# Queries and keys as further columns of the values' projection, brought to their rows through DRAM

## The chip, the core and the metric

The kernel runs on one core of a Trainium2 chip. A core has TensorE (PE: matmuls, with its weight loads listed as PEld), VectorE (DVE), ScalarE (ACT), GpSimd (POOL) and SyncE (SP, which here only issues DMAs), a 128-partition SBUF, and PSUM with 8 banks, into which matmuls write. The metric is the device time of one execution in microseconds.

## What is computed

Two layers work on x of shape (4, 64, 96, 96) in fp32. The first is an attention over all 9216 positions of an image, with a sigmoid in place of a softmax; the second multiplies a few Fourier modes by weights. The change concerns the first.

```python
# layer 0, on xn = _gn(x); C = 64, C8 = 8, N = 96 * 96 = 9216
q = jnp.einsum('bchw,oc->bohw', xn, wq) + bq      # 8 channels
k = jnp.einsum('bchw,oc->bohw', xn, wk) + bk      # 8 channels
v = jnp.einsum('bchw,oc->bohw', xn, wv) + bv      # 64 channels
energy = jnp.einsum('bcn,bcm->bnm', Q, K)
att = jax.nn.sigmoid(energy)
out = jnp.einsum('bcm,bnm->bcn', V, att) + xn
scale = jax.nn.sigmoid(mlp(out.mean) + mlp(out.max))
x = x + out * scale
# layer 1
x = x + irfft2(modes of rfft2(_gn(x)), mixed over channels)
```

## The kernel before

The four images are worked on as two pairs; the channels of a pair's two images fill the 128 partitions of `xs[p]`. The positions of a pair are cut into 18 blocks of 512. Each block is in turn a query tile (512 columns), and against each query tile stand 144 tiles of keys: 72 groups of 128 positions for each of two images. So 2 x 18 x 144 = 5184 tiles are worked through, each in three steps: an energy matmul into one PSUM bank (L481), a sigmoid on ScalarE over three or four banks at a time (L500), and the values times these attentions on TensorE (L517).

**Rows of queries and keys.** An energy matmul contracts over 32 rows: 8 channels, four times, since each of query and key is split into a high and a low part so that products of fast-format numbers (float32r) give fp32 accuracy. Four such groups of 32 rows lie in 128 partitions (two images, twice). The projection matrices `wq` and `wk` have the 8 columns repeated so that a matmul puts them at once into all rows. `keys(p, s)` (L428) projects one block into a bank, and `halves` and `low_or_high` (L406, L407, L416) make the high part in some rows and the rest in others, into `kT`. `queries` (L452) does the same for a query tile, and copies halves to the other rows (L462). `values_of` (L439, L443) projects the values of a block with x as the stationary operand, into `vT`.

**Order.** A planner runs ahead of the work (`while len(done) < len(sizes)`) and cuts the tiles into bursts of seven (six where a bank is needed elsewhere). For each burst t it writes down which steps come with it: `together[t]` (projections, which use banks of the next burst that are free for a moment), `alone[t]` (one step with a bank of its own) and `ends[t]` (steps without a bank). The loop below then emits: the energies of burst t+1, the values for the older tiles, the sigmoids of burst t+1, some more values, the projections, the rest. The order on PE, ACT and DVE is this one by hand (`manual_schedule`); the order on SP's queue is left to the scheduler of the framework, and each queue works in order. SP's DMAs carry one of eight completion semaphores in turn, so that a DMA waits for the one eight before it.

Pair 0's keys and values are projected during its first query tile: `keys(0, s)` and `values_of(0, s)` come shortly before the energies of block s. Pair 1's are projected during the last query tile of pair 0, as the old keys and values are finished with (`renewed`). A query tile is projected 42 tiles ahead (`AHEAD`). During pair 1 the second layer of pair 0 is worked in between (`second_layer`, class `Hidden`), with many DMAs on SP's queue (L269 to L381). The tail is the second layer of pair 1.

Of the kernel before, what the change touches and what calls it, by code (L numbers as in the profile page):

```python
# [33 lines left out]
F32 = mybir.dt.float32  # L34
# [19 lines left out]

SIZE, HEAD = 7, 3
AHEAD = 6 * SIZE
ALL = NPAIR * NBLK * TILES
# [12 lines left out]

FIRST = {"wq": P, "wk": P, "wv": P, "pav": P, "bq": 1, "bk": 1, "low": 2, "nhalf": 1, "bv": P}
SECOND = {"w1": 2 * R, "w2": P, "ident": P, "fw": 2 * KW, "fh": 4 * KH, "gh": 2 * H, "gw": 4 * W}
# [11 lines left out]
def tile_kernel(ctx: ExitStack, tc: tile.TileContext, x, cst, late, spec, out):  # L84
# [24 lines left out]
    def named(name, rows=P):  # L109
        return cs[:rows, PLACE[name]]  # L110
# [273 lines left out]
    with tc.tile_pool(name="work", bufs=1) as work, \  # L384
# [10 lines left out]

        kT = kvp.tile([P, NCH // 2, P], F32R, tag="kT", name="kT")

# [3 lines left out]
        def halves(src, bias, name):  # L401

            shape = [P, src.shape[-1]]
            u = qp.tile(shape, F32, tag="full", name=f"full_{name}", bufs=1)
            h = qp.tile(shape, F32R, tag="high", name=f"high_{name}")
            nc.vector.tensor_scalar(u, src, bias, None, ALU.add)  # L406
            nc.vector.tensor_copy(h, u)  # L407
            return u, h
# [5 lines left out]
        def low_or_high(dst, u, h, is_low):  # L414

            mark[0] = nc.vector.scalar_tensor_tensor(dst, h.bitcast(F32), is_low, u,  # L416
                                                     ALU.mult, ALU.add)
# [5 lines left out]
        def keys(p, s):  # L423
            pp = bank_a(f"pk_{p}_{s}")
            src = xs[p][:, bass.ts(s, NB)].rearrange("p (a e m) -> p e a m", e=2, m=P)
            for e in range(2):
                cols = bass.ts(e, P // 2)
                projected[0] = nc.tensor.matmul(pp[cols, :NB // 2], named("wk")[:, cols],  # L428
                                                src[:, e, :, :], start=True, stop=True)
            ku, kh = halves(pp[:, :NB // 2], named("bk"), f"k_{p}_{s}")  # L430
            low_or_high(kT[:, 2 * s:2 * s + 2, :].rearrange("p a m -> p (a m)"), ku, kh,
                        low_sb[:, 1:2])

        def values_of(p, s):
            pp = bank_a(f"pv_{p}_{s}")

            for i in range(4):
                for e in range(2):
                    projected[0] = nc.tensor.matmul(  # L439
                        pp[bass.ts(e, P // 2), bass.ts(i, P)],  # L440
                        xs[p][:, bass.ts(2 * (4 * s + i) + e, P // 2)], named("wv"),
                        start=True, stop=True)
            nc.vector.tensor_tensor(  # L443
                vT[:, 4 * s:4 * s + 4, :], pp.rearrange("p (i m) -> p i m", m=P),
                named("bv").unsqueeze(1).to_broadcast([P, 4, P]), ALU.add)

        def queries(p, n):
            pq = bank_a(f"pq_{p}_{n}")
            half = NB // 2
            for e in range(2):  # L450
                rows = bass.ts(e, P // 2)
                projected[0] = nc.tensor.matmul(  # L452
                    pq[rows, :half], named("wq")[:, rows],
                    xs[p][:, n * NB + e * half:n * NB + (e + 1) * half], start=True, stop=True)
            qu, qh = halves(pq[:, :half], named("bq"), f"q_{p}_{n}")
            q = qp.tile([P, NB], F32R, tag="q", name=f"q_{p}_{n}")
            for e in range(2):
                rows, cols = bass.ts(e, P // 2), bass.ts(e, half)
                low_or_high(q[rows, cols], qu[rows, :], qh[rows, :], low_sb[rows, 0:1])
                for b in range(2):  # L460
                    to, of = 64 * (1 - e) + 32 * b, 64 * e + 32 * b
                    nc.vector.tensor_copy(q[to:to + 32, cols], q[of:of + 32, cols])  # L462
            return q
# [13 lines left out]
        def energies(t):  # L477

            for i in range(total[t] - sizes[t], total[t]):
                r = 32 * (i % 4)  # L480
                nc.tensor.matmul(banks[:, bank_of(i), :], kT[r:r + 32, i // 4 % (NCH // 2), :],  # L481
                                 ask[i // TILES][r:r + 32, :], start=True, stop=True)
# [4 lines left out]
        def parts(t):  # L487

            for lo, part in ((0, order[t][:HEAD]), (HEAD, order[t][HEAD:])):
                if part:  # L490
                    yield 7 * (t % 2) + lo, min(part), len(part)
# [93 lines left out]
        norm0[0]()  # L585
        norm0[1]()
        keys(0, 0)
        warm_behind()
        q = first_queries()
        warm_behind()  # L590
        values_of(0, 0)
        warm_behind()

# [73 lines left out]
        kept = [TILES * (NPAIR * NBLK - 1) + 2 * (STRIP // P) * (s + 1) for s in range(NSTRIP)]  # L667
        ask, asked, known, valued, renewed, again_at = {0: q}, 1, 2, 2, 0, 0
        sizes, total, order, done, block, edges = [6], [6], [list(range(1, 7))], [], [], set()
        way = 1  # L670
        while len(done) < len(sizes):

            t, was = len(done), done[-1] if done else 0
            n = max(1, -(-was // TILES))
            edge = TILES * n
            crossing = edge < ALL and edge < total[t] - 3
            block.append(n if crossing else n - 1)
# [12 lines left out]
            elif total[t] < ALL:  # L690
                steps = together.setdefault(t, [])
                while known < NBLK and known <= (total[t] + 2 * SIZE - 1) // 8:
                    steps.append(lambda s=known: keys(0, s))
                    if known + 1 < NBLK:
                        end(t, norm0[known + 1])
                    known += 1
                while valued < NBLK and valued <= (total[t] + 2 * SIZE - LAG) // 8:
                    steps.append(lambda s=valued: values_of(0, s))
                    valued += 1
                if renewed < NBLK and was >= TILES * (NBLK - 1) + 8 * (renewed + 1):  # L700
                    steps.append(lambda s=renewed: keys(1, s))
                    steps.append(lambda s=renewed: values_of(1, s))
                    renewed += 1
                if asked < NPAIR * NBLK and total[t] + AHEAD >= TILES * asked and t not in alone:
                    steps.append(lambda n=asked: ask.update({n: queries(n // NBLK, n % NBLK)}))
                    asked += 1
                assert len(steps) <= HEAD
                while chain and not steps and t not in alone:
                    own, step, wait, since = chain[0]
                    if t < max(ready[0] + wait, started[0] + since):  # L710
                        break
                    if own:
                        alone[t] = step
                    elif own is None:
                        end(t, step)
                    else:
                        steps.append(step)
                    ready[0] = t
                    chain.pop(0)
# [6 lines left out]
            if crossing:  # L726
                way = 1 if n % 2 else -1
            elif together.get(t - 1):
                way = -way
            order.append(list(free)[::way][:ALL - total[t]])  # L730
            sizes.append(len(order[-1]))
            total.append(total[t] + sizes[-1])
            done.append(total[-1] - LAG if crossing else min(edge, total[-1] - LAG))
            while again_at < NSTRIP and done[t] >= kept[again_at]:
# [9 lines left out]

        spare[0] = 0
        energies(0)
        sigmoids(0)
        later(norm0[2])
        keys(0, 1)
        warm_behind()  # L750
        values_of(0, 1)
        with tc.manual_schedule(engines=ENGINES):
            put_off = []
            for t in range(T):
# [9 lines left out]
                if t + 1 < T:  # L764
                    sigmoids(t + 1)
                at_work = next((i for i in range(old, len(items)) if sum(
                    c.stop - c.start for _, c in items[:i]) >= 2 * NB), len(items))
                attend(items[old:at_work])
                for i, step in enumerate(together.get(t, ())):
                    spare[0] = order[t + 1][i]  # L770
                    step()
# [192 lines left out]
def _constants(l0):  # L964
# [24 lines left out]
    for b in range(2):  # L989
        rows = slice(b * C, (b + 1) * C)  # L990
        a[rows, PLACE["wv"].start + b * C:PLACE["wv"].start + (b + 1) * C] = l0["wv"].T
        a[rows, PLACE["w1"].start + b * R:PLACE["w1"].start + (b + 1) * R] = l0["ca_w1"].T
        a[b * R:(b + 1) * R, PLACE["w2"].start + b * C:PLACE["w2"].start + (b + 1) * C] = \
            l0["ca_w2"].T
# [52 lines left out]
```

## Time and profile before

| What | Value |
|---|---|
| median of 3 runs | 3081.17 us (3081.09 to 3081.43) |
| the profiled execution | 3080.95 us, span 3079.2 us |
| granted TensorE clock, mean | 0.997 |
| L500 sigmoids, x1503 | 2394.5 us busy |
| L517 values times attentions, x11824 | 2408.3 us busy |
| L481 energies, x5040 (and x144 of the first tile) | 544.7 us (and 17.1) busy |
| queue q1 (SP): packets, MB | 72000, 71.57 |

A row of the groups gives the line of the code, the engine, the operation, what it writes and reads with shapes, how often it occurs, the busy time, the mean of one in ns, and the idle time of the engine just before such instructions with what ended it. An fp32 matmul is two records, and matmuls on different columns or rows of the array run at the same time, so busy time is less than count times mean. The timeline gives start, duration, engine and operation of merged instructions; SPq is SP's queue, where the duration of a DMA row is the time that SP needs to issue it, not that of the transfer. The first query tile ends at 134.9 us (the first row of L523) and the second at 214.92; the last one of pair 0 runs from 1406.30 to 1508.07.

### The profile page before, as it was taken

What the parts mean: (1) busy time and instruction counts of PE and PEld (TensorE: products, weight loads), DVE (VectorE), ACT (ScalarE), POOL (GpSimd) and SP (SyncE); (2) the same over time, 40 slices, a digit from 0 to 9 for tenths busy, and PEclk for the clock granted to TensorE, in tenths of its full rate; (3) what the DMA queues carried; (4) which work ended last, traced back from release to release, by engine and by line L of the source; (5) the groups of instructions that cost most, each with busy time, mean ns of one, the idle gap of its engine ahead of it and who ended that gap; (6) DMA issues with size and microseconds to landing.
All of it is one profiled execution on the core that took longest, in us unless ns stands there. A gap on an engine that the chain in (4) does not pass through costs nothing.

```text
span 3079.2 us, 42720 instructions
## 1 busy us (share of the span) xinstructions
PE 3055.0 (99%) x19022; PEld 1145.5 (37%) x19022; DVE 387.2 (13%) x818; ACT 2417.3 (79%) x1543; POOL 27.1 (1%) x52
## 2 busy tenths in 40 slices
PE   8999999999999999999999999999999999999998
PEld 4433333333333333334433333333333333333336
DVE  4300000000000000002312111100110000000005
ACT  4688888888888888887688887777777888888872
POOL 0000000000000000000000000000001000000001
PEclk9999999999999999999999999999999999999999
DMA  3000000000000000000122322412113000000027
GB/s 145 1 1 1 1 1 1 1 1 1 1 1 1 1 1 1 1 1 1 31 75 61 84 74 77 132 24 29 50 44 131 1 1 1 1 1 1 5 63 246
DMA packets 80490, 99.48 MB, mean 32 GB/s; under 512 B 48209, under 2 KB 58193, under 8 KB 80209
## 3 DMA queue, kind: packets, MB, share of 16 engines
q1 hardware_dynamic: 72000, 71.57, 8.0%
q0 software_dynamic: 5776, 20.45, 1.9%
q10 hardware_dynamic: 2528, 4.72, 0.4%
q8 instruction: 149, 2.44, 0.3%
q14 instruction: 37, 0.29, 0.0%
HBM read 67.49 MB, written 28.05 MB: 31 GB/s over the span
## 4 chain that ended last, share of the span: by engine, by line
PE 98%; DVE 1%; ACT 1%; DMA 0%; issue 0%; SPq 0%; DVEq 0%; ACTq 0%
PE banks L517 75%; PE banks L481 16%; PE banks L439 1%; PE banks L428 1%; PE banks L206 1%; PE banks L376 1%; ACT at L500 0%; PE banks L452 0%; PE py L955 0%; PE pv L206 0%; DMA x<-in_x_dram 0%; PE pa L857 0%; PE banks L354 0%; PE idle_I-15036_15051 L820 0%; PE pu L869 0%
## 5 line engine op out<-in xcount | busy, mean ns | idle before, releaser
L500 ACT ACTIVATE at<-banks 128x1536 f32<-128x1536 f32 x1503 | 2394.5, 1640 | 590.6 <-PE banks L481 564.3
L517 PE MATMUL banks<-at,vT 128*64 128x512 f32 (+1 forms) x11824 | 2408.3, 546 | 0.0
L517 PEld LDWEIGHTS banks<-at,vT 128*64 128x64 f32 x11824 | 780.3, 136 | 1338.6 <-issue 1280.1
L481 PE MATMUL banks<-q,kT 32*128 32x512 f32 x5040 | 544.7, 453 | 2.6 <-ACT at L500 2.5
L481 PEld LDWEIGHTS banks<-q,kT 32*128 32x128 f32 x5040 | 223.6, 183 | 453.8 <-ACT at L500 340.0
L406 DVE TENSOR_SCALAR full_q<-banks,cs 128x256 f32<-128x256 f32 x35 | 16.9, 483 | 1361.0 <-PE banks L452 1361.0
L523 DVE SCALAR_TENSOR_TENSOR x<-banks,x 128x512 f32<-128x512 f32 x36 | 24.9, 692 | 648.9 <-PE banks L517 648.9
L462 DVE CAST q<-q 32x256 fp32r<-32x256 f32 x140 | 39.9, 285 | 3.8
L439 PE MATMUL banks<-cs,x 128*64 128x128 f32 x576 | 37.7, 273 | 0.4 <-DVE at L471 0.4
L379 DVE TENSOR_TENSOR x<-banks,x 128x384 f32<-128x384 f32 x24 | 13.4, 558 | 188.0 <-PE banks L376 186.1
L439 PEld LDWEIGHTS banks<-cs,x 128*64 128x64 f32 x576 | 33.8, 137 | 7.3 <-issue 0.9
L416 DVE SCALAR_TENSOR_TENSOR q<-high_q,cs,full_q 64x256 fp32r<-64x256 f32 x70 | 33.6, 480 | 1.8
L406 DVE TENSOR_SCALAR full_k<-banks,cs 128x256 f32<-128x256 f32 x36 | 17.4, 484 | 115.6 <-PE banks L428 89.8
L443 DVE TENSOR_TENSOR vT<-banks,cs 128x512 f32<-128x512 f32 x36 | 24.7, 685 | 9.7 <-PE banks L439 9.7
L525 DVE TENSOR_REDUCE maxs<-x 128x1 f32<-128x512 f32 x36 | 24.7, 686 | 1.2
L619 DVE COPY ws<-banks 128x512 f32<-128x512 f32 x16 | 11.1, 692 | 95.7 <-PE banks L206 95.6
L531 DVE BATCH_NORM_STATS2 stats<-x 128x6 f32<-128x512 f32 x36 | 22.2, 680 | 6.0 <-DMA x<-in_x_dram 5.8
L428 PE MATMUL banks<-x,cs 128*64 128x256 f32 x144 | 22.3, 388 | 0.2 <-DVE x L152 0.2
L570 PE MATMUL banks<-x 128*128 128x256 f32 (+1 forms) x46 | 14.9, 470 | 6.3 <-DMA x<-in_x_dram 6.3
L452 PE MATMUL banks<-x,cs 128*64 128x256 f32 x140 | 21.1, 379 | 0.0
L481 PE MATMUL banks<-q_first,kT 32*128 32x512 f32 x144 | 17.1, 463 | 2.8 <-DVE kT L416 1.7
L376 PE MATMUL banks<-cs,ws 128*64 128x384 f32 x96 | 19.6, 486 | 0.0
(133 smaller groups left out, 467.8 us busy)
## 6 DMA issues: line engine op xcount, KB each, us to landing
ws<-in_spec_dram SPq DMA_DIRECT2D x20, 512.0 KB
x<-in_x_dram SPq DMA_DIRECT2D x14, 512.0 KB
room<-in_spec_dram SPq DMA_DIRECT2D x12, 512.0 KB
w<-in_spec_dram POOLq DMA_DIRECT2D x10, 512.0 KB, 6.8
old<-in_x_dram SPq DMA_DIRECT2D x12, 384.0 KB
x1d<-x SPq DMA_DIRECT2D x12, 384.0 KB
xd<-old SPq DMA_DIRECT2D x12, 384.0 KB
xT<-xd SPq DMA_DIRECT2D x36, 128.0 KB
```

The costliest lines, as they stand in the source:

```text
L206: self.last = nc.tensor.matmul(pv[bass.ts(g, 32), :].rearrange("q (n k o) -> q n k o", n=SIDE, o=C)[:, :, k, :], self.ut[:, at:at + 32], s ...
L376: nc.tensor.matmul(py[bass.ts(b, C), :4 * W], self.z[:, i, bass.ts(b, C)], named("gw"), start=True, stop=True)
L406: nc.vector.tensor_scalar(u, src, bias, None, ALU.add)
L416: mark[0] = nc.vector.scalar_tensor_tensor(dst, h.bitcast(F32), is_low, u, ALU.mult, ALU.add)
L428: projected[0] = nc.tensor.matmul(pp[cols, :NB // 2], named("wk")[:, cols], src[:, e, :, :], start=True, stop=True)
L439: projected[0] = nc.tensor.matmul(pp[bass.ts(e, P // 2), bass.ts(i, P)], xs[p][:, bass.ts(2 * (4 * s + i) + e, P // 2)], named("wv"), star ...
L443: nc.vector.tensor_tensor(vT[:, 4 * s:4 * s + 4, :], pp.rearrange("p (i m) -> p i m", m=P), named("bv").unsqueeze(1).to_broadcast([P, 4, P ...
L462: nc.vector.tensor_copy(q[to:to + 32, cols], q[of:of + 32, cols])
L481: nc.tensor.matmul(banks[:, bank_of(i), :], kT[r:r + 32, i // 4 % (NCH // 2), :], ask[i // TILES][r:r + 32, :], start=True, stop=True)
L500: nc.scalar.activation(at[:, of:of + n, :], banks[:, bank:bank + n, :], AF.Sigmoid)
L517: attended[0] = nc.tensor.matmul(acc[half, cols], vT[:, j, half], at[:, place(2 * pair + b), cols], start=(j == 0), stop=(j == NCH - 1 and ...
L523: nc.vector.scalar_tensor_tensor(blk, acc, 1.0, blk, ALU.mult, ALU.add, accum_out=sums[p][:, m:m + 1])
```

## The change

The stationary operand of the values' projection is x itself. The change appends 32 columns to the moving matrix `wv`: queries and keys (8 columns each) of both images. So the values' projection of a block also gives its queries and keys, but turned: positions in partitions, channels along the free axis. VectorE adds the bias (`u`), makes high and low parts (`t`) and turns squares of 32 by 32 (`turned`). Four DMAs on SP write `turned` to a DRAM buffer `split`; sixteen DMAs read from it into the rows of `kT` (`known_keys`) and sixteen into the rows of a query tile (`queries`), each for 8 rows. `keys` by matmul stays for blocks 0 to 6 of pair 0 (`DIRECT`), `first_queries` for the first tile, and the values of block 0 of pair 0 are projected without the new columns. The stationary operands of `values_of` and of `energies` now take every second column. `u`, `t` and `turned` have one buffer each. `values_of` takes two banks, and the planner's steps carry the number of their banks; its rules for what is attended in a burst are changed a little, and pair 0's blocks are normalized two ahead.

```diff
 SIZE, HEAD = 7, 3
+DIRECT = 7
...
+QK = 4 * C8
+FIRST = {"wq": P, "wk": P, "wv": P + QK, "pav": P, "bq": 1, "bk": 1, "low": 2, "nhalf": 1,
+         "bv": P, "bqk": QK}
...
-        kT = kvp.tile([P, NCH // 2, P], F32R, tag="kT", name="kT")
+        kT = kvp.tile([P, NBLK, NB // 2], F32R, tag="kT", name="kT")
+        split = [dram.tile([NBLK, QK, 2, NB], F32, tag=f"qk{p}", name=f"qk_{p}") for p in range(NPAIR)]
...
-        def values_of(p, s):
-            pp = bank_a(f"pv_{p}_{s}")
-
-            for i in range(4):
-                for e in range(2):
-                    projected[0] = nc.tensor.matmul(
-                        pp[bass.ts(e, P // 2), bass.ts(i, P)],
-                        xs[p][:, bass.ts(2 * (4 * s + i) + e, P // 2)], named("wv"),
-                        start=True, stop=True)
+        def values_of(p, s, width=P + QK):
+
+
+            pp = banks[:, spare[0]:spare[0] + 2, :2 * width].rearrange(
+                "p h (a m) -> p h a m", a=2)
+            src = xs[p][:, bass.ts(s, NB)].rearrange("p (a m h) -> p a h m", a=2, h=2)
+            for h in range(2):
+                for a in range(2):
+                    for e in range(2):
+                        projected[0] = nc.tensor.matmul(
+                            pp[bass.ts(e, P // 2), h, a, :], src[:, a, h, bass.ts(e, P // 2)],
+                            named("wv")[:, :width], start=True, stop=True)
...
+            if width == P:
+                return values()
+            u = qp.tile([P, 2, 2, QK], F32, tag="u", name=f"u_{p}_{s}", bufs=1)
+            t = qp.tile([P, 2, 2, 2, QK], F32R, tag="t", name=f"t_{p}_{s}", bufs=1)
             nc.vector.tensor_tensor(
-                vT[:, 4 * s:4 * s + 4, :], pp.rearrange("p (i m) -> p i m", m=P),
-                named("bv").unsqueeze(1).to_broadcast([P, 4, P]), ALU.add)
+                u, pp[:, :, :, P:].rearrange("p h a m -> p a h m"),
+                named("bqk").unsqueeze(1).unsqueeze(1).to_broadcast([P, 2, 2, QK]), ALU.add)
+            values()
+            nc.vector.tensor_copy(t[:, 0], u)
+            nc.vector.tensor_tensor(t[:, 1], u, t[:, 0].bitcast(F32), ALU.subtract)
+            turned = qp.tile([P, 2, 2, NB // 8], F32, tag="turned", name=f"turned_{p}_{s}", bufs=1)
+            nc.vector.transpose(turned.rearrange("p l a (m h) -> p (l a) h m", h=2),
+                                t.rearrange("p l a h m -> p (l a) h m").bitcast(F32))
+            for g in range(4):
+                nc.sync.dma_start(
+                    split[p][s].rearrange("r l (a g m) -> g r (l a) m", a=2, g=4)[g],
+                    turned[bass.ts(g, QK)].rearrange("r l a m -> r (l a) m"))
+
+        def known_keys(p, s):
+
+            for r in range(4):
+                of = split[p][s].rearrange("(b t o) l (a m) -> b t a l o m", b=2, t=2, a=2)[
+                    r % 2, 1, r // 2]
+                for half in range(2):
+                    for twice in range(2):
+                        to = 32 * r + 16 * half + C8 * twice
+                        nc.sync.dma_start(kT[to:to + C8, s, :].bitcast(F32), of[half])
 
         def queries(p, n):
...
             q = qp.tile([P, NB], F32R, tag="q", name=f"q_{p}_{n}")
-            for e in range(2):
-                rows, cols = bass.ts(e, P // 2), bass.ts(e, half)
-                low_or_high(q[rows, cols], qu[rows, :], qh[rows, :], low_sb[rows, 0:1])
-                for b in range(2):
-                    to, of = 64 * (1 - e) + 32 * b, 64 * e + 32 * b
-                    nc.vector.tensor_copy(q[to:to + 32, cols], q[of:of + 32, cols])
+            for r in range(4):
+                of = split[p][n].rearrange("(b t o) l m -> b t l o m", b=2, t=2)[r % 2, 0]
+                for twice in range(2):
+                    for half in range(2):
+                        to = 32 * r + 16 * twice + C8 * half
+                        nc.sync.dma_start(q[to:to + C8, :].bitcast(F32), of[half])
             return q
...
-                nc.tensor.matmul(banks[:, bank_of(i), :], kT[r:r + 32, i // 4 % (NCH // 2), :],
+                nc.tensor.matmul(banks[:, bank_of(i), :],
+                                 kT[r:r + 32, i % TILES // 8, :].rearrange(
+                                     "r (m h) -> r h m", h=2)[:, i // 4 % 2],
                                  ask[i // TILES][r:r + 32, :], start=True, stop=True)
...
-                while known < NBLK and known <= (total[t] + 2 * SIZE - 1) // 8:
-                    steps.append(lambda s=known: keys(0, s))
...
+                if known < DIRECT and known <= (total[t] + 2 * SIZE - 1) // 8:
+                    steps.append((1, lambda s=known: keys(0, s)))
                     known += 1
-                while valued < NBLK and valued <= (total[t] + 2 * SIZE - LAG) // 8:
-                    steps.append(lambda s=valued: values_of(0, s))
+                while (valued < min(NBLK, (total[t] + 4 * SIZE - 1) // 8 + 1)
+                       and sum(n for n, _ in steps) <= 2):
+                    steps.append((2, lambda s=valued: values_of(0, s)))
+                    if valued >= DIRECT:
+                        end(t, lambda s=valued: known_keys(0, s))
                     valued += 1
...
                 if renewed < NBLK and was >= TILES * (NBLK - 1) + 8 * (renewed + 1):
-                    steps.append(lambda s=renewed: keys(1, s))
-                    steps.append(lambda s=renewed: values_of(1, s))
+                    steps.append((2, lambda s=renewed: values_of(1, s)))
+                    end(t, lambda s=renewed: known_keys(1, s))
                     renewed += 1
-                if asked < NPAIR * NBLK and total[t] + AHEAD >= TILES * asked and t not in alone:
-                    steps.append(lambda n=asked: ask.update({n: queries(n // NBLK, n % NBLK)}))
+                if asked < NPAIR * NBLK and total[t] + AHEAD >= TILES * asked:
+                    end(t, lambda n=asked: ask.update({n: queries(n // NBLK, n % NBLK)}))
                     asked += 1
```

## The prediction

> **What bounds the kernel now.** I read the first two parts of the page first, then the chain, then the groups.
>
> ```profile
> PE 3055.0 (99%) x19022; PEld 1145.5 (37%) x19022; DVE 387.2 (13%) x818; ACT 2417.3 (79%) x1543; POOL 27.1 (1%) x52
> ...
> PE 98%; DVE 1%; ACT 1%; DMA 0%; issue 0%; SPq 0%; DVEq 0%; ACTq 0%
> ...
> L481 PE MATMUL banks<-q,kT 32*128 32x512 f32 x5040 | 544.7, 453 | 2.6 <-ACT at L500 2.5
> ...
> L439 PE MATMUL banks<-cs,x 128*64 128x128 f32 x576 | 37.7, 273 | 0.4 <-DVE at L471 0.4
> ...
> L428 PE MATMUL banks<-x,cs 128*64 128x256 f32 x144 | 22.3, 388 | 0.2 <-DVE x L152 0.2
> ...
> L452 PE MATMUL banks<-x,cs 128*64 128x256 f32 x140 | 21.1, 379 | 0.0
> ```
>
> The kernel is TensorE from end to end: PE carries 98% of the chain, and the 5040 energy matmuls wait 2.6 us in all. So TensorE work that is taken away shortens the kernel one for one, as long as nothing else becomes late. L439 (values), L428 (keys) and L452 (queries) are the three projections.
>
> Next the timeline of TensorE in a plain stretch: one round of seven tiles goes from one row of energies to the next.
>
> ```profile
> 1000.98 0.73 PE L481 MATMUL banks<-q,kT 32*128 32x512 f32 x7
> ...
> 1004.80 0.73 PE L481 MATMUL banks<-q,kT 32*128 32x512 f32 x7
> ```
>
> 3.82 us for 7 tiles: 0.546 a tile, 4.37 for the eight tiles that one block of keys or values serves. TensorE never rests there.
>
> Last the timeline of SP, whose queue gets the new transfers.
>
> ```profile
> 1828.09 1.79 SPq L310 DMA_DIRECT2D ad<-ae  x4
> 1831.27 0.31 SPq L314 DMA_DIRECT2D ah<-ad  x1
> ```
> ```profile
> 2065.98 1.42 SPq L362 DMA_DIRECT2D ws<-zd  x4
> ```
> ```profile
> 2031.23 1.72 SPq L244 DMA_DIRECT2D room<-vd  x4
> ```
>
> A DMA occupies SP for about as long whatever its size: four stores of 64 KB in 1.79 us (0.45 each), four loads from DRAM in 1.42 or 1.72 (0.36 to 0.43 each). A load that needs what was just stored waits for the landing: the last of the four stores began near 1829.43, and the load starts at 1831.27, 1.84 us later; the same sum for the stores before room<-vd gives 2.07. I take 1.9.
>
> **What the Trainium skill says.** "DMA: Bandwidth & Descriptors", section "Anatomy of one DMA", has a fixed cost of about 2 us, most of it the receipt of the write; the 1.84 and 2.07 us here agree. The same page, "Issuing engines are not separate DMA queues", calls the sequencer's time to start a DMA "usually small relative to the DMA itself"; here it is 0.36 to 0.45 us apiece, and with some twenty DMAs in a row it is the larger part. "SBUF — State Buffer", in its note on cachelines, says a step of up to four fp32 can be read free of charge; no row of this trace has a step of two. "TensorE: Matmul & The Clock Gate", section "What's actually happening", says an idle window of about 3.4 us halves the clock; the page here shows nines in every slice and cannot tell.
>
> **The change part by part.**
>
> *TensorE's saving.* L428 falls from 144 records to 28 (keys by matmul remain for 7 of 36 blocks): 22.3 x 116/144 = 18.0 us gone. L452 goes: 21.1. L439 moves 160 columns in place of 128 in 35 of 36 blocks: 37.7 x 35/36 x 0.25 = 9.2 more. Net 30 us less. The bursts of tiles stay as many (1503 sigmoids in the built program before and after, with the same shapes), so energies, sigmoids and attended values cost the same.
>
> *The steps of two* in the stationary operand (every second column of kT and of x): taken as free, by the page on SBUF. From above: L955 loads 32x128 weights with a step of 32 elements in 306 ns, against 183 for L481. If step two cost that too, 0.12 us a burst in some 750 bursts, 92 us.
>
> *Waits on TensorE.* The built program has 402 more wait-only instructions there (16 loads behind each query tile, 16 behind each kT block). The trace has a time for one such instruction, on the queue of VectorE: 21 ns, so 8 us for all. I take 0, since the queue reads ahead and L481 shows 2.6 us idle although many of its instructions wait twice.
>
> *VectorE.* A block adds u, a cast, a subtraction and a transpose; by the lengths of rows of like shape (0.35 + 0.25 + 0.35 + 0.45) 1.4 us. Removed are three instructions (1.26 us) of 29 key blocks and eight of 35 query blocks (0.483 + 0.294 + 2 x 0.480 + 4 x 0.285 = 2.88 us). It is 13% busy; its time counts for nothing, but its order does, below.
>
> *SP.* Per block of 512 positions: 4 stores of `turned`, then for kT 16 loads that wait for all four stores; per query tile 16 loads. That is 1164 more DMAs in one in-order queue. The program lets eight be in flight (each waits for the one eight before); 8 x 0.40 = 3.2 us is more than a landing, so this does not bind. One block with keys costs SP
>
> 3 x 0.45 + 1.9 (landing) + 16 x 0.40 = **9.65 us**,
>
> and TensorE reaches the next block after 4.37 + 1.31 (values, 37.7/36 x 1.25) = **5.68 us**. SP becomes the bound wherever blocks of keys follow each other: twice.
>
> *First stretch, pair 0, blocks s = 7 to 17 of the first query tile.* In the built order, between values_of(0,7) and the first energy on kT block 7 stand 16 attended tiles' worth and 17 energies, two more value blocks and one key block: 16 x 0.546 + 2 x 1.31 + 0.62 = 12.0 us. From there to block 17 it is 10 x 5.68: 69 us. By SP: 2.5 us of VectorE until `turned` is there, ten periods (96.5), and for the last block 1.35 + 1.9 + 15 x 0.40 + 1.9 = 11.2: 110 us. TensorE stands for 110 - 69 = **41 us**. Query tile 1 is loaded in the gaps before s = 7 and is in nobody's way.
>
> *Second stretch, pair 1's blocks s = 0 to 17, projected during the last query tile of pair 0.* Its keys are wanted a whole query tile (144 tiles, 79 us) later, so lateness of kT alone would be covered. But `turned` is a single buffer: the transpose of block s+1 waits until the stores of block s have landed, those stores queue on SP behind the 16 loads of block s-1, and behind the transpose on VectorE stand the next block's reads of PSUM, which hold two banks that TensorE's next burst of energies needs. So TensorE can be only about two blocks ahead of SP. Last block: by SP 2.5 + 15 x 9.65 + 1.35 + 1.9 (stores of block 15 landed) + 1.5 (transpose, u, values) = 152 us after values_of(1,0); without waits 17 x 5.68 + 2 = 99. **53 us**. The loads of query tiles 18 and 19 between them (three at a time) fall into the landing wait.
>
> *Other query tiles.* 16 x 0.40 = 6.4 us of SP, asked for 42 tiles (23 us) ahead: hidden in blocks 2 to 17. From block 19 on the queue also holds the second layer's DMAs (L278 to L381), some of which wait tens of us for VectorE or TensorE; in the built order the last load of each query tile stands behind steps that come 10 or more bursts (40 us) before it is needed, and the weights of L346 are asked for two steps ahead. Nothing, or up to 6 us each time if that cover failed.
>
> Sum against the profiled execution (3080.95 us, span 3079.2; the median 3081.17 is 0.2 more): 3081 - 30 + 41 + 53 = **3145 us**.
>
> **The rivals.**
>
> A. SP keeps pace and the saving remains. The sum depends on the load's issue time p: 16 loads in 10 + 1 periods of the first stretch and 15 of the second make 416 us per us of p, so the 64 us of net loss vanish at p = 0.25 us. For it: the new loads have 8 descriptors only, and the 16 DMA engines are idle in both stretches (1 GB/s). Against: 16 descriptors a load at L244 took as long as 128. Then 3051 to 3075.
>
> B. Only the first stretch stalls, as the single buffer of the second is covered somewhere: 3081 - 30 + 41 = 3092.
>
> C. It gets worse than the sum: the strided weights cost their 92 us (3237), or TensorE's clock falls in the pauses of 4 us a period. Halved for good, its work of 5.68 becomes 11.36 us a period, over 9.65, and 26 periods cost 44 us more: 3189.
>
> D. The projection does not do what it says: too much stays of the old one. The counts above exclude it beyond the 7 key blocks already taken.
>
> **How the numbers follow.** Main case 0.68, with its own range 3111 (p = 0.33, the time of a lone DMA, with landing as taken: 64 - 29 = 35, and 5 less) to 3170 (p = 0.44 and stores at 0.5). A 0.12, B 0.10, C 0.10. The range 3088 to 3192 takes in B and the clock. About 0.2% (6 us) is what a measurement of this kernel can tell from no change. Faster is A without its upper end, 0.10; no change 0.03; slower 0.87.
>
> **What would show it.** Right: TensorE's busy share falls in the slices of the first 190 us and between 1430 and 1600 and nowhere else; in the first stretch energies wait for DMAs into kT, in the second VectorE's transpose waits for DMAs into `qk`; SP issues without a pause there, about 10 us a block; PE busy falls by some 30 us. Wrong: a pitch of kT's loads below 0.25 us; TensorE's pauses in other stretches (query tiles late, then waits on q); energies longer in plain stretches than 3.82 us a round (strided weights).

## The result

The changed kernel takes 3176.36 us (median of 4 runs, 3172.63 to 3178.96) against 3081.30 for the kernel before on the same chip: 1.0307 times as long, 95% interval 1.0289 to 1.0325. The forecast was 3145 with a range of 3088 to 3192; the direction and the two places of the loss came out as written, its size was 31 us short. The traces below are of single executions: 3178.96 us, the longest of the four, against 3080.95 before.

The page of the changed kernel, first parts and chain:

```profile
span 3177.2 us, 43832 instructions
...
PE 3098.3 (98%) x18772; PEld 1172.5 (37%) x18772; DVE 287.5 (9%) x591; ACT 2421.5 (76%) x1543; POOL 27.2 (1%) x52
...
PE   8799999999999999999799999999999999999999
...
PEclk9899999999999999999899999999999999999998
...
PE 91%; SPq 5%; DMA 2%; DVE 1%; issue 1%; ACT 0%; DVEq 0%; POOL 0%; ACTq 0%
```

In the chain SP's queue holds 5% and DMAs 2%, where there was 0% before: SP has become part of what sets the end. TensorE's row of slices (79.4 us each) has a seven in the second slice and one in the 20th, and nowhere else; the granted clock (PEclk) has an eight in the same two. The starts of the rows that add a finished query tile to x (L523 before, L555 after) give the length of each query tile:

| us | before | changed |
|---|---|---|
| end of query tile 1 of pair 0 | 134.9 | 182.8 |
| tiles 2 to 17 of pair 0, together | 1271.4 | 1269.7 |
| tile 18, the last of pair 0 | 101.8 | 148.4 |
| tile 1 of pair 1 | 82.9 | 90.9 |
| tiles 2 to 18 of pair 1, together | 1403.2 | 1401.5 |

So 47.9 us were lost in the first tile, 46.6 in the 18th and 8.0 in the 19th (tile 1 of pair 1). In the other 33 tiles only 1.7 + 1.7 us were gained.

The timeline of SP in the first stretch of the changed kernel:

```profile
93.02 2.48 SPq L470 DMA_DIRECT2D qk<-turned  x4
97.00 5.34 SPq L482 DMA_DIRECT2D kT<-qk  x16
102.44 2.48 SPq L470 DMA_DIRECT2D qk<-turned  x4
106.32 5.34 SPq L482 DMA_DIRECT2D kT<-qk  x16
```

Four stores, a pause until they have landed, sixteen loads, and at once the next stores: SP waits for nothing here but its own landing. The first loads of block 7 start at 66.50 us and those of block 17 at 165.13, so one block takes 9.86 us.

What TensorE and VectorE waited for, in the first stretch (60 to 183 us; us in total, times, longest) and then in the second (1452 to 1601 us):

```profile
PE banks L510 <- DMA kT<-qk: 24.1, 25, 2.5
```
```profile
PE banks L510 <- DVE vT L451: 27.1, 10, 4.7
```
```profile
DVE turned L467 <- DMA qk<-turned: 98.5, 14, 8.4
```

In the first, the energies wait for their keys. In the second no energy waits for a key: it waits for VectorE's reading of a bank (L451), which stands behind a transpose that waits up to 8.4 us for the only `turned` to be stored. The longest of these, in VectorE's and then TensorE's timeline:

```profile
1515.31 0.45 DVE L467 STREAM_TRANSPOSE turned<-t 128x256 f32<-128x256 f32 x1 [8.40 <-DMA qk<-turned]
1515.68 0.25 DVE L460 TENSOR_TENSOR u<-banks,cs 128x128 f32<-128x128 f32 x1
1515.85 0.67 DVE L451 TENSOR_TENSOR vT<-banks,cs 128x512 f32<-128x512 f32 x1
```
```profile
1516.58 0.79 PE L510 MATMUL banks<-q,kT 32*128 32x512 f32 x2 [4.67 <-DVE vT L451]
```

The groups show one more thing: the energies' busy time rose, and so did the mean of one of their weight loads (the kernel before first, L481, then the changed one, L510):

```profile
L481 PEld LDWEIGHTS banks<-q,kT 32*128 32x128 f32 x5040 | 223.6, 183 | 453.8 <-ACT at L500 340.0
```
```profile
L510 PE MATMUL banks<-q,kT 32*128 32x512 f32 x5040 | 564.2, 459 | 34.4 <-DVE vT L451 27.1
L510 PEld LDWEIGHTS banks<-q,kT 32*128 32x128 f32 x5040 | 247.3, 190 | 490.6 <-ACT at L532 347.5
```

A weight load takes 190 ns in place of 183. The reader is to keep this for the run with contiguous operands below.

### The profile page after: what moved, and what is told of

Its sections match the earlier page's. It is cut to its first block, busy times and chain, and to the rows that moved or that the text cites. A ratio compares the mean times of both kernels' runs of the same rounds, so it can differ in the third digit from the quotient of the medians.

```text
span 3177.2 us, 43832 instructions
## 1 busy us (share of the span) xinstructions
PE 3098.3 (98%) x18772; PEld 1172.5 (37%) x18772; DVE 287.5 (9%) x591; ACT 2421.5 (76%) x1543; POOL 27.2 (1%) x52
## 2 busy tenths in 40 slices
DMA packets 117042, 117.18 MB, mean 37 GB/s; under 512 B 76560, under 2 KB 90256, under 8 KB 116752
## 4 chain that ended last, share of the span: by engine, by line
PE 91%; SPq 5%; DMA 2%; DVE 1%; issue 1%; ACT 0%; DVEq 0%; POOL 0%; ACTq 0%
PE banks L549 71%; PE banks L510 16%; SPq L482 3%; DMA qk<-turned 2%; SPq L470 2%; PE banks L209 1%; PE banks L379 0%; PE py L1001 0%; PE pv L209 0%; DMA x<-in_x_dram 0%; PE banks L446 0%; PE pa L903 0%; PE banks L357 0%; PE idle_I-15827_15842 L866 0%; PE pu L915 0%
## 5 line engine op out<-in xcount | busy, mean ns | idle before, releaser
L510 PE MATMUL banks<-q,kT 32*128 32x512 f32 x5040 | 564.2, 459 | 34.4 <-DVE vT L451 27.1
L510 PEld LDWEIGHTS banks<-q,kT 32*128 32x128 f32 x5040 | 247.3, 190 | 490.6 <-ACT at L532 347.5
L555 DVE SCALAR_TENSOR_TENSOR x<-banks,x 128x512 f32<-128x512 f32 x36 | 24.9, 691 | 2014.1 <-PE banks L549 1938.7
L510 PE MATMUL banks<-q_first,kT 32*128 32x512 f32 x144 | 29.4, 496 | 26.3 <-DMA kT<-qk 24.1
L446 PEld LDWEIGHTS banks<-cs,x 128*64 128x64 f32 x576 | 42.7, 148 | 24.7 <-issue 17.2
L446 PE MATMUL banks<-cs,x 128*64 128x160 f32 (+1 forms) x576 | 47.9, 310 | 0.8 <-DVE x L155 0.8
L467 DVE STREAM_TRANSPOSE turned<-t 128x256 f32<-128x256 f32 x35 | 15.7, 448 | 156.9 <-DMA qk<-turned 156.1
L510 PEld LDWEIGHTS banks<-q_first,kT 32*128 32x128 f32 x144 | 12.2, 194 | 47.3 <-issue 34.7
L451 DVE TENSOR_TENSOR vT<-banks,cs 128x512 f32<-128x512 f32 x36 | 24.5, 679 | 0.1
L903 PE MATMUL pa<-xt,lc 128*128 128x256 f32 x72 | 16.9, 386 | 1.1 <-DVE xt L895 1.1
```

Source lines behind the costliest of these rows:

```text
L446: projected[0] = nc.tensor.matmul(pp[bass.ts(e, P // 2), h, a, :], src[:, a, h, bass.ts(e, P // 2)], named("wv")[:, :width], start=True, s ...
L451: nc.vector.tensor_tensor(vT[:, 4 * s:4 * s + 4, :].rearrange("p (h a) m -> p h a m", h=2), pp[:, :, :, :P], named("bv").unsqueeze(1).unsq ...
L510: nc.tensor.matmul(banks[:, bank_of(i), :], kT[r:r + 32, i % TILES // 8, :].rearrange("r (m h) -> r h m", h=2)[:, i // 4 % 2], ask[i // TI ...
L555: nc.vector.scalar_tensor_tensor(blk, acc, 1.0, blk, ALU.mult, ALU.add, accum_out=sums[p][:, m:m + 1])
```

## The experiments

Theory: the issue of DMAs on one queue is the bound in both stretches, directly through the keys in the first and through the single buffer in the second. Rivals: the transfers themselves (landing, bytes) are too slow whoever issues them; the lateness of the keys, not the buffer, stops the second stretch; the waits at TensorE cost the time. All changes are edits of the changed kernel; times of the kernel before beside these runs lie between 3080.9 and 3081.3 us.

**Fewer, larger loads.** The two copies of eight rows by one DMA:

```diff
-                for half in range(2):
-                    for twice in range(2):
-                        to = 32 * r + 16 * half + C8 * twice
-                        nc.sync.dma_start(kT[to:to + C8, s, :].bitcast(F32), of[half])
+                for half in range(2):
+                    one = of[half]
+                    two = bass.AP(tensor=one.tensor, offset=one.offset,
+                                  ap=[[0, 2], [2 * NB, C8], [1, NB // 2]])
+                    to = 32 * r + 16 * half
+                    nc.sync.dma_start(kT[to:to + 16, s, :].bitcast(F32), two)
```

> The two equal copies of eight key rows are read by one DMA of 16 rows (the source repeated), so a kT block takes 8 loads in place of 16. If SP's issue time is the bound (0.33 us a load in the changed kernel), its period falls from 9.86 to 7.2 us: the first query tile shortens by about 27 us (ends near 156), the last one of pair 0 by about 40 us (148.4 to 108), 3105 us in all. If the landing of transfers or the bytes were the bound, the period would stay near 9.9 and the time at 3176. If the waits at TensorE were the cost, half of a few us would go: 3165 to 3175.

Measured: 3169.13 us, ratio 1.0283 (1.0265 to 1.0300); the first tile ends at 178.2, the last of pair 0 takes 146.7. The theory's number was missed by 64 us. SP's timeline in this run says why:

```profile
94.18 5.10 SPq L484 DMA_DIRECT2D kT<-qk  x8
99.37 2.51 SPq L470 DMA_DIRECT2D qk<-turned  x4
103.27 5.10 SPq L484 DMA_DIRECT2D kT<-qk  x8
```

Eight loads take 5.10 us, 0.64 each, where sixteen of half the rows took 5.34, 0.33 each. SP is still never idle but for the landing. What failed was my assumption that a DMA costs SP the same whatever its form; that the queue is the bound is not touched by this, nor shown. The repeated source is not what doubles it: the loads of the next run, 16 rows without a repeat, take 0.63 each.

**The query tiles' loads halved too**, one DMA for high and low rows together, `nc.sync.dma_start(q[to:to + 16, :].bitcast(F32), of)`, in place of two, on top of the edit above:

> As the run with 8 loads for kT, and the query tiles too take 8 loads in place of 16. The plain query tiles tell what their waits cost TensorE: if each waiting instruction costs TensorE time, the longer round at the start of a query tile (4.1 to 4.3 us against 3.83 in the changed kernel) falls by half of the excess, some 0.2 us in 33 tiles, so about 6 us below the run with kT alone: 3098. If the waits are free, the two runs agree within their noise.

Measured: 3170.80 us, ratio 1.0290 (1.0274 to 1.0305), the same as the run before it within their noise; by the whole time the waits would be free, as the expectation has it. The tiles say otherwise. The sixteen plain tiles of pair 0 take 1267.4 us together against 1269.6 in the run with kT alone, 0.14 us less each, and tiles 2 to 18 of pair 1 take 1.6 less. But the 18th and 19th take 2.9 and 3.1 us more than there (149.6 and 91.0), for a reason that was not looked for, and that hides the gain. The records behind this are waiting instructions ahead of the energies, on the queue of TensorE's weight loads; the changed kernel first, then this run (count, then shortest, median and longest in ns):

```profile
L510 PEldq EVENT_SEMAPHORE  x441: 51/51/1261, 59.2 to 3011.2; - x147
```
```profile
L511 PEldq EVENT_SEMAPHORE  x232: 51/51/51, 60.6 to 3003.5; - x116
```

Each of the first four energies of a query tile waits for four DMAs, of which two waiting instructions carry the surplus: eight times 51 ns in the changed kernel, 0.41 us, and four times in this run. In the changed kernel's timeline such rounds take between 4.09 and 4.29 us where a plain one takes 3.83. So these waits are not wholly hidden.

**Sixteen places for `turned`**, all DMAs as they were:

```diff
+        room_for_turned = work.tile([P, 2 * KW * P], F32, tag="ah", name="room_for_turned")
...
-            turned = qp.tile([P, 2, 2, NB // 8], F32, tag="turned", name=f"turned_{p}_{s}", bufs=1)
+            turned = room_for_turned[:, bass.ts(s % 16, NB // 2)].rearrange(
+                "p (l a m) -> p l a m", l=2, a=2)
```

> turned gets 16 places (in a tile that the second layer needs only later), with all DMAs as in the changed kernel. If the single buffer is what ties TensorE to SP in the second stretch, the last query tile of pair 0 falls from 148.4 to about 100 us, and the lateness moves to the next one, where keys and the second layer's DMAs come late (90.9 to between 95 and 110); the first stretch changes by 0 to -20 us, through the order on SP alone. 3120 to 3145 in all. If the lateness of the keys themselves stops TensorE there, the tile stays near 148 and the time near 3176.

Measured: 3138.35 us, ratio 1.0186 (1.0171 to 1.0202); the first tile ends at 167.1, the 18th takes 130.6, the 19th 83.1. All that TensorE's matmuls waited for in the second stretch (1430 to 1560 us) is now

```profile
PE banks L513 <- DMA kT<-qk: 21.2, 1, 21.2
PE banks L513 <- DMA q<-qk: 7.0, 3, 5.9
```

The ten waits for VectorE are gone, so the single buffer did tie TensorE to SP. But SP still needs 8.4 us a block, more than TensorE, and the lateness came back as one wait of 21.2 us for keys and 7.0 for a query tile, at the first energies of pair 1, inside the 18th tile's time and not in the 19th, where I had put it. The first stretch gained 15.6 us: in SP's timeline most stores of a block now stand ahead of the loads of the one before, the pauses for the landing are nearly gone, and a block takes 8.6 us in place of 9.86.

**The loads of keys on GpSimd's queue**, `nc.gpsimd.dma_start(kT[...])` in `known_keys`, the same transfers:

> The 16 loads of a kT block are issued by GpSimd, which is idle; stores and queries stay on SP. GpSimd takes about 0.53 us a DMA in the kernel before, so 8.5 us a block. If the issue of one queue is the bound: the first query tile shortens by about 14 us (10 periods of 8.5 in place of 9.86, ends near 169), the last tile of pair 0 has no stall any more (stores alone take 2.5 + 1.9 us a block) and falls to about 97 us, the next to about 83: 3103 us in all. If the transfers themselves were too slow, whoever issues them, it would stay at 3176.

Measured: 3108.82 us, ratio 1.0090 (1.0075 to 1.0105); the first tile ends at 168.9, the 18th takes 98.0, the 19th 84.6. GpSimd's timeline in the first stretch:

```profile
66.26 42.04 POOL L482 DMA_DIRECT2D kT<-qk  x80 [46.29 <-DMA qk<-turned]
109.25 24.92 POOL L482 DMA_DIRECT2D kT<-qk  x48 [0.95 <-DMA qk<-turned]
```

Eighty DMAs in 42.04 us, 0.53 each, 8.4 a block: the first stretch is now bound by GpSimd, and the second, where keys have time, is free. The bytes moved are those of the changed kernel (117.20 MB against 117.18) and the packets are more (124465 against 117042), and yet 68 us went. That excludes the rival of slow transfers. What it takes from SP is both the issue of the loads and their place in one order with the stores and the landing; it does not part the two.

**Keys of pair 0 by matmul again**, `DIRECT = 18`:

> All 18 key blocks of pair 0 are projected by matmul again (11 more key projections of 0.62 us); its queries, and all of pair 1, still come through DRAM. If the first stretch's stall is the kT loads on SP, the first query tile falls from 182.8 to about 139 us and the rest stays: 3132 us. If its stall had another cause (the order of the planner, the stores, VectorE), it stays above 160.

Measured: 3136.42 us, ratio 1.0177 (1.0164 to 1.0191); the first tile ends at 140.0, the 18th still takes 148.5. With the loads of kT gone from the first stretch its stall is gone too, to within some 5 us (134.9 in the kernel before), of which the wider value projections account for about 4, an estimate (17 blocks by 0.26 us, less one query projection of 0.6); the second stretch is untouched by this.

**Contiguous stationary operands**, by another order of the positions in a block:

```diff
-            src = xs[p][:, bass.ts(s, NB)].rearrange("p (a m h) -> p a h m", a=2, h=2)
+            src = xs[p][:, bass.ts(s, NB)].rearrange("p (a h m) -> p a h m", a=2, h=2)
...
-                                     "r (m h) -> r h m", h=2)[:, i // 4 % 2],
+                                     "r (h m) -> r h m", h=2)[:, i // 4 % 2],
```

> Keys and values are ordered so that every stationary operand is contiguous again; the stores of turned fall into 256 pieces of 128 B in place of 128 of 256 B. If the step of two costs TensorE, the plain round goes from 3.83 back to 3.82 us, the mean weight load of the energies from 190 to 183 ns, and the 16 plain query tiles of pair 0 from 1269.6 us in all to about 1266.5; nothing of this if it is free. The two stretches stay or lengthen with the stores: 3165 to 3190 in all.

Measured: 3173.01 us, ratio 1.0297 (1.0283 to 1.0311). The group of the energies' weight loads in this run:

```profile
L510 PEld LDWEIGHTS banks<-q,kT 32*128 32x128 f32 x5040 | 235.8, 182 | 494.4 <-ACT at L532 373.2
```

182 ns against 190, and the sixteen plain tiles take 1267.3 us against 1269.7. So the step of two is nearly but not quite free: 0.15 us a tile, an estimate of 5 us over 36 tiles. The stores in pieces of 128 B take SP 2.51 us, as the larger ones.

**Both stalls removed**, twice. First with the two simplest edits, `DIRECT = 18` and the keys of pair 1 on GpSimd:

> Both stalls taken away in the simplest way: keys of pair 0 by matmul, kT loads of pair 1 on GpSimd. From the runs with each alone: first query tile 139 (134.9 in the kernel before), last of pair 0 98 (101.8), the rest as with GpSimd: 3079 us, the same as before within 4 us. The 30 us less of TensorE's work are then given back as 7 for the keys, and about 9 for waits on query tiles and 5 for strided weights, which leaves a gain of a few us at most.

Measured: 3078.57 us, ratio 0.9992 (0.9984 to 1.0000); first tile 137.2, 18th 98.0. Then with the loads of a block shared by two queues, `(nc.sync if half else nc.gpsimd).dma_start(...)`, the sixteen places, and pair 0's values three bursts earlier (`7 * SIZE` in place of `4 * SIZE`):

> The kT loads of a block half on SP, half on GpSimd, 16 places for turned, and the values of pair 0 projected three bursts earlier. SP then has 2.5 + 8 x 0.33 = 5.2 us a block, GpSimd 4.2, both under TensorE's 5.7. If issue on one queue is all that bound, both stalls go: first query tile 131 to 142, last of pair 0 96 to 100, 3060 to 3075 us in all, faster than before. If something else lies right behind it (landing, VectorE, banks), the first tile stays above 150.

Measured: 3078.32 us, ratio 0.9990 (0.9982 to 0.9998); first tile 139.9, 18th 97.7. Both stalls went, but not down to the 3060 to 3075 expected. In the run with shared loads the waits of its matmuls in the first stretch (26 to 140 us) are 5.0 us in all, and its rounds there carry 89 waiting instructions of 51 ns.

**The small costs removed as well.** Both kernels with contiguous operands and 8 loads for a query tile:

> The run with kT's loads split over SP and GpSimd, with contiguous stationary operands (5 us less by the runs before) and 8 loads for a query tile (half of the waiting instructions at its first round, 0.13 us in 34 tiles, 4 us less): 3069 us, 0.4% below before. If the two savings overlap or the loads of queries hit other stretches, 3073 to 3078.

> The run with pair 0's keys by matmul and pair 1's kT loads on GpSimd, with the same two edits: 3069 us by the same sum; its first query tile has no wait for kT loads (88 waiting instructions of 51 ns less than the other run) but 11 key projections more, so the two should lie within 4 us of each other.

Measured: 3068.80 us, ratio 0.9963 (0.9949 to 0.9977), and 3069.33 us, ratio 0.9960 (0.9948 to 0.9973), as expected. The page of the first:

```profile
PE 3044.6 (99%) x18772; PEld 1145.0 (37%) x18772; DVE 288.8 (9%) x591; ACT 2418.0 (79%) x1543; POOL 146.0 (5%) x284
```

TensorE is the bound again, with 10 us less of busy time than in the kernel before. These two are faster than both kernels, by 0.4% against the one before.

## Why the prediction came out as it did

By stretches, the forecast of +64 us is +38 in the first tile, +46.5 in the second stretch and -20 in the 33 tiles without a stall. The profiled executions have +47.9, +54.6 and -3.4. So the mechanism was right in both stretches and the sum too small in each of them, but the largest error, half of the shortfall, lies in the tiles where nothing stands.

*TensorE's saving, 30 us*: the size was right for the projections (L446 47.9 us busy where 37.7 + 9.2 was written; L452 gone, L431 at 28 records), but most of it was given back by the two steps below that I had taken as free. The sign that I had named for it, PE busy some 30 us lower, did not come: it rose from 3055.0 to 3098.3 us. With both stalls removed it is 3054.5, still no lower, and 3044.6 with the small costs removed as well.

*SP's period, 9.65 us*: measured 9.86 in the first stretch. That the sum came so near is luck, as its terms were wrong in both directions: a store took 0.62 us where I took 0.45, a load 0.33 where I took 0.40, and from the start of the last store to the first load it was 2.5 us on average where I took 1.9. The reading behind the issue time, that it is the same whatever the size, came from DMAs of 64 to 256 KB only. The upper end of the main case is also added up wrongly: p = 0.44 with stores at 0.5 gives 3166, not 3170.

*First stretch*: 41 us of standing, less 3.0 us of smaller projections after block 0 (11 key blocks and a query projection fewer, 17 value blocks wider: -6.8 - 0.6 + 4.4 = -3.0), is 38 net; measured 47.9. The period accounts for 2 of the 10 that are missing. Another 3 are a late start: the loads of block 7 begin 8.96 us after its value projection (57.54 to 66.50) where the prediction has 2.5 + 1.35 + 1.9 = 5.75, as the transposes already wait for stores there. Two more come behind the last wait for a key, at 169.15 us, when the values' matmuls run at a granted clock of 0.61; here beside the same work at 1.00:

```profile
169.84 5.23 PE L549 MATMUL banks<-at,vT 128*64 128x256 f32 x16
179.49 3.23 PE L549 MATMUL banks<-at,vT 128*64 128x256 f32 x16
```

The rest, under 3 us, stays unassigned; the 88 waiting instructions for kT blocks (11 blocks, eight each), 51 ns apiece, would be up to 4.5, by count and not by a run of their own.

*Second stretch*: 53 us less 18 times (0.62 - 0.26) is 46.5 net. That tile 18 alone lost 46.6 is a coincidence: in both kernels the last two of pair 1's 18 value blocks are projected in tile 19 (at 1606.62 and 1611.65 us in the changed kernel), so the forecast has to be held against both tiles, 54.6. I had followed the stretch to the reading of the last value block, 152 us after the start of the first projection; measured 154.7 (1459.20 to 1613.9). Against the run with keys on GpSimd, where the two tiles take 182.6 us together and nothing stands, the stall is 56.7, near the 53. So of the 8 us that are missing some 4 are a longer stall and some 4 are saving that did not come; tile 19 has 112 waiting instructions ahead of its energies. What I had not followed is the order on VectorE behind the last transposes: energies wait 4.4 us for L555 and 2.5 for the gate's L587 there. That one buffer and VectorE's order are the mechanism is shown by the run with sixteen places.

*Waits on TensorE*: the step that failed most plainly. I took 0, with 8 us at most, from a 21 ns record of VectorE; on TensorE one takes 51 ns, and ahead of a query tile they are not hidden. The 33 tiles without a stall gained 3.4 us in place of 33 x 0.60 = 20, so 0.50 us a tile is missing; halving the query loads recovered 0.14 us a tile and contiguous operands 0.15, together more than half of it. What the rest of the waits costs was not measured.

*The steps of two*: taken as free from "SBUF — State Buffer", the note on cachelines; measured 190 against 183 ns a load. The statement of the page holds nearly (a step of 32 costs 306 ns), and the measurement decides: about 5 us. The sign named for it, plain rounds longer than 3.82 us, showed only as 3.83.

*The rivals.* A failed: SP's pitch was 0.33, above the 0.25 at which it would have decided. B did not hold, since the buffer was not covered. D did not either, by the counts above. Of C, the weights cost 5 and not 92 us. The clock did fall, to 0.86 of full speed between 60 and 183 us and 0.90 between 1452 and 1601, and was 1.00 in both stretches in the run with shared loads. "TensorE: Matmul & The Clock Gate", section "What's actually happening", gives one idle window of about 3.4 us as enough to halve it; single waits reached 4.7 us in the second stretch, but only 2.5 in the first, so that figure alone does not explain the first. No run separates what the clock cost beyond the 2 us above: while TensorE waits for SP, a slower TensorE need not cost anything.

## What to carry to other kernels

Before a computation is replaced by transfers, add up what the issuing queue needs for them: here twenty small DMAs and the landing between them took 9.9 us of SP per block, more than the TensorE work of 5.7 that went on beside it, while the DMA engines were 12% busy. A single buffer between an engine and such a queue hands the queue's pace on to everything that stands behind it in that engine's order. And a tile that is assembled by many DMAs is paid for again at the reader: half as many loads per query tile made a plain tile 0.14 us shorter here.

## What was not expected of the hardware

- A load of 16 rows took SP 0.63 or 0.64 us, with or without a repeated source, one of 8 rows 0.33; joining two DMAs saved SP next to nothing (5.10 us in place of 5.34). The stores in 128 or 256 pieces took 0.62 and 0.63.
- A waiting instruction of TensorE's queue takes 51 ns in the median, one of VectorE's 21.
- A stationary fp32 operand with a step of two elements loads in 190 ns, contiguous in 182 or 183, with a step of 32 in 306.
